# Routing operands of the later groups made tile by tile inside the shared expert's stages, first loads in program order, and the last two batches' rows stored by GpSimd, in a one-core adapter and mixture-of-experts kernel

## The chip, the core and the metric

The kernel runs on one core of a Trainium2 chip. A core has five engines with queues of their own: PE (matrix products), DVE (vector operations), ACT (casts, copies, activations), POOL (here mostly indirect transfers) and SP (which only issues transfers). Each engine works through its instructions in the order fixed when the kernel is built; an instruction that waits for a semaphore holds back all behind it on the same engine. The metric is the device time of one execution in microseconds, lower is better.

## The reference

Two parts in a row: a per-batch adapter product, then a feed-forward layer with a shared expert and 16 routed experts, of which each token uses two. The result is added to `x`.

```
x: (8, 256, 1024) f32;  itok: adapter id per batch (8 of them, here 3 to 7)
y = einsum('bsi,boi->bso', x, cond_weight[itok])        # 8 x [256,1024] x [1024,1024]
t = y.reshape(2048, 1024)
shared = (silu(t @ sg.T) * (t @ su.T)) @ shared_down.T   # 1024 -> 1024 -> 1024
p = softmax(t @ gate_w.T)                                # 16 experts
v, i = top_k(p, 2);  v = v / sum(v)
moe = sum over the two experts e in i of  v_e * ((silu(t @ g_e.T) * (t @ u_e.T)) @ w_down_e.T)   # inner size 256
out = x + shared + moe
```

The 2048 rows of `t` are handled as four groups of 512 rows (two batches each).

## The kernel before, in words

**Precision.** Every large fp32 operand is split into a high part (an ACT cast, L84) and a low remainder (a DVE subtraction, L85); `split` does both. `mm3` (L133) then makes a product out of three matmuls, high x high (L134), high x low (L135) and low x high (L136). So each operand costs one ACT and one DVE instruction of about 1.0 and 1.2 us per 128x1024 tile, and PE runs three matmuls for one product.

**Loads.** `load_w` (L114) issues one 512 KB load on SP into one of the `wst` staging buffers and splits it into one of five `whl` buffers; PE frees such a buffer with its last matmul on it. After each load `load_w` takes one entry from the hand-written list `between`, if there is one, and runs it right behind that split: this is how small pieces of other work are put among the large products. `held` and `after_loads` likewise tie work behind the last split or the last load. A scheduler at build time fixes the order on each engine, within those ties.

**First part of the span.** Twenty matmuls on a constant tile come first (L149). Then `cond(b)` for b = 0 to 7 makes the adapter product of a batch: two tiles of `xT` and eight weight tiles, 96 matmuls, copies of the sums into `yrow` by ACT (L270), and two stores of these rows to `y_d` in DRAM (L272, on ACT's queue). `load_first` (L100) cuts the first two tiles of batch 0 into halves so that PE may start sooner. `constants` (L171) fills small tables on POOL and DVE. The rows come back by POOL's fetch `yr<-y_d` (L394) and a DVE stream transpose (L218, `turned(b, k)` in the list), into `raw` for groups 0 and 1, and for groups 2 and 3 into `tt`.

**The shared expert's gate and up products** of groups 0 and 1 are made with a seven-product (Strassen-like) scheme, class `Up`, in stages a, b, c and d of four steps u each; `product` (L503) makes 24 matmuls of 128x512 a time. Stage c adds to copies of `X` put into the accumulators by ACT (`seeded`), its result goes into `G` by L574; stage d adds into `X` on DVE (L585), which also frees accumulators. Stage c needs the operand `t4`, stage d needs `t1` and `b22`, each two tiles of a ring (`operand_half`, L398). The stages alternate with `cond(4)` to `cond(7)`.

**Routing.** For each group the logits are 32 matmuls on operands that for groups 2 and 3 are made from `tt` into `whl` buffers named `rb`, in two halves (k = 0 and 1, one batch each) by `half_works` (L412): `operands` makes both tiles of a half, `products` runs its 16 matmuls (L278). `choices(g)` then runs `route` (L287): softmax and top two on DVE, rank matmuls `rk` (L339 to L349), places for each row. `scatter(g)` writes eight columns of row numbers to a table in DRAM with POOL's indirect transfers (L378).

**Behind the last group.** Experts are sorted by count on DVE, one indirect read brings the table back (L891, `cr`), a DVE transpose and addition make the row indices `ix` (L898), and POOL gathers the experts' rows with one indirect transfer per quarter tile (L805, in `expert_rows`). Meanwhile `shared_down` (L620) makes the shared expert's down product of groups 0 and 1. Each of the two has the rows of `x` loaded into `acc` tiles (L615; group 0 on SP's queue, group 1 on POOL's), adds the accumulators to them on DVE (L641), which frees the accumulators, and stores the sum (L642). After that come the 16 experts, then the shared expert for groups 2 and 3 and the last sums.

The order around the change is the program at the end of the kernel: `cond(5)`, stage b steps 2 and 3, `cond(6)`, stage c steps 0 and 1, `cond(7)`, stage c 2 and 3, stage d 0 to 3, `scatter(3)`.

Of the kernel before, what the change touches and what calls it, by code (L numbers as in the profile page):

```python
# [1 line left out]

# [8 lines left out]
FR = mybir.dt.float32r  # L11
# [6 lines left out]
P = 128  # L18
# [21 lines left out]
def adapter_moe_kernel(ctx: ExitStack, tc: tile.TileContext, xT, x, itok, wc, gate, wgu, wd, sgu, sd, out):  # L40
# [39 lines left out]

    last_cast, last_split, last_load = [None], [None], [None]

    def split(hi, lo, src):
        last_cast[0] = nc.scalar.copy(hi, src).ins  # L84
        last_split[0] = nc.vector.tensor_tensor(lo, src, hi.bitcast(F32), op=ALU.subtract).ins  # L85
        return last_split[0]


    def held(*works):
        with tc.issue_after(last_split[0]):  # L90
            for work in works:
                work()
# [21 lines left out]
    def load_w(src, staged=(wst, "wst")):  # L114
        st = staged[0].tile([P, 1024], F32, tag=staged[1], name="st")
        loads[0] += 1
        hl = homes[loads[0] % len(homes)].tile([P, 2, 1024], FR, tag="whl", name="hl")
        last_load[0] = nc.sync.dma_start(st, src)
        end = split(hl[:, 0, :], hl[:, 1, :], st)
        work = between.pop(0) if between else None  # L120
        if work:
            with tc.issue_after(end):
                work()
        return hl

    def after_loads(work):
        def later():
            with tc.issue_after(last_load[0].ins):
                work()

        return later
# [14 lines left out]

    nc.gpsimd.memset(ones, 1.0)
    warm = psm.tile([P, 4, P], F32, tag="sm", name="warm")
    for k in range(20):  # L149
        nc.tensor.matmul(warm, ones, ones[:, :].rearrange("p (o n) -> p o n", o=1).to_broadcast([P, 4, P]), start=True, stop=True)  # L150


# [85 lines left out]
    def cond(b, rows, staged=(wst, "wst")):  # L238
        aid = []

        def weights(k):
            if not aid:
                aid.append(nc.values_load(it_sb[0:1, b : b + 1], engines=(mybir.EngineType.SP,), min_val=0, max_val=NA - 1))
            return wc[ds(aid[0], 1), k].rearrange("a p f -> p (a f)")

        if b == 0:
            x0, w0 = load_first(lambda: xT[b, :, 0, :], lambda: weights(0), staged)
            xt = [x0]
        else:
            xt, w0 = [load_w(xT[b, :, 0, :], staged)], None  # L250
        yrow = [rows.tile([P, 1024], F32, tag="yrow", name=f"yrow{k}") for k in range(2)]
        for h in range(2):
            ps = [bank() for k in range(2)]
            for q in range(4):
                if h == 0 and q == 2:
                    xt.append(load_w(xT[b, :, 1, :], staged))
                w = w0 if w0 and h == q == 0 else load_w(weights(h * 4 + q))
                for k in range(2):
                    for ci in range(2):
                        c = 2 * q + ci  # L260
                        xv = xt[c // 4].rearrange("p l (c s) -> p l c s", c=4)
                        mm3(
                            ps[k],
                            [xv[:, l, c % 4, k * P : (k + 1) * P] for l in range(2)],
                            [w[:, l, ci * 512 : (ci + 1) * 512] for l in range(2)],
                            c == 0,
                            c == NC - 1,
                        )
            for k in range(2):
                nc.scalar.copy(yrow[k][:, h * 512 : (h + 1) * 512], ps[k])  # L270
        for k in range(2):
            nc.scalar.dma_start(y_d[2 * b + k].rearrange("a p f -> p a f"), yrow[k][:, :].rearrange("p (a f) -> p a f", a=4))  # L272


    def route_part(lp, n0, get, n):
        for c in range(NC):
            for l in range(2):
                nc.tensor.matmul(  # L278
                    lp[:, n0 : n0 + n],
                    gpk[:, c * 2 * E : c * 2 * E + P],  # L280
                    get(c)[l],
                    start=(c == 0 and l == 0),
                    stop=(c == NC - 1 and l == 1),
                )
# [86 lines left out]
    def scatter(g):  # L371
        with tc.issue_after(last_rows[0]):
            scatter_now(g)
# [29 lines left out]
    def operand(ring, src):  # L403
        return [operand_half(ring, src, k) for k in range(2)]
# [7 lines left out]
    def half_works(g, k, src):  # L412
        t = []

        def operands():
            for q in range(2):
                rb = whl.tile([P, 2, 4, 2 * P], FR, tag="whl", name="rb")
                split(rb[:, 0], rb[:, 1], src[:, 4 * q : 4 * q + 4, :])
                t.append(rb)

        def products():
            if k == 0:
                lps[g] = logits()
            with tc.issue_after(last_product[0]):
                route_part(lps[g], k * 2 * P, lambda c: [t[c // 4][:, l, c % 4, :] for l in range(2)], 2 * P)

        return operands, products

    def choices(g):
        return lambda: route(g, lps[g])  # L430

# [7 lines left out]
    def logits():  # L439
        return psm.tile([P, GT], F32, tag="sm", name="lp")  # L440

    def both(*works):
        def work():
            for w in works:
                w()

        return work
# [2 lines left out]

    class Up:
        def __init__(self, first, raw, X, S, G, ring, ys, g0):
            self.first, self.raw, self.X, self.S, self.G, self.ring, self.ys, self.g0 = first, raw, X, S, G, ring, ys, g0
            if first:
                s, at = ([a[:, 2 * k : 2 * k + 2, :].rearrange("p a n -> p (a n)") for k in range(a.shape[1] // 2)] for a in (S, self.half(0, 0)))
                self.spare = [s, s, s[2:] + at, [s[3]] + at + [None]]
# [96 lines left out]
        def stage_b(self, u, made=False):  # L553
# [8 lines left out]
            for m in range(2):  # L562
                self.product(ps[m], w2, m, self.t3, False)
                nc.scalar.copy(self.X[:, 2 * u + m, :], ps[m])

        def stage_c(self, u):
            if u == 0:
                self.t4 = operand(self.ring, self.half(1, 0))
            w = load_w(sgu[1, 1, u])
            ps = self.seeded(u)  # L570
            for m in range(2):
                f = 2 * u + m
                self.product(ps[m], w, m, self.t4, False)
                nc.vector.tensor_tensor(self.G[:, f, :], self.G[:, f, :], ps[m], op=ALU.mult)  # L574

        def stage_d(self, u):
            if u == 0:
                self.t1 = operand(self.ring, self.half(0, 1))
                self.b22 = operand(self.ring, self.half(1, 1))
            w1, w2 = load_w(ss_d[0, u]), load_w(ss_d[3, u])  # L580
            ps = [bank() for m in range(2)]
            for m in range(2):
                f = 2 * u + m
                self.product(ps[m], w1, m, self.t1, True)
                nc.vector.tensor_tensor(self.X[:, f, :], ps[m], self.X[:, f, :], op=ALU.add)  # L585
            if u:
                self.end_d()
            self.open = u, ps, w2
            if u == 3:
                self.end_d()  # L590
# [360 lines left out]
    def fetch_rows(b, dst):  # L951
        def work():
            rows[b] = batch_rows(b, ys, dst)

        return work

    def turned(b, k):
        return lambda: rows[b][k]()

    cond(0, ys, early)  # L960
    fetch_rows(0, up.place(0, 0))()
    constants(ring)
    cond(1, ys, early)
    between[:] = [turned(0, 0), None, both(turned(0, 1), fetch_rows(1, up.place(0, 1))), after_loads(lambda: tables(ring))]
    cond(2, ys)
# [25 lines left out]
    cond(4, ys)  # L991
    tv = tt.rearrange("p k (b n) -> p (k b) n", b=4)
    fetch_rows(4, tv)()
    h0, h1 = half_works(2, 0, tv), half_works(2, 1, tv)
    up.sums_operands()
    between[:] = [None, choices(1)]
    up.stage_b(0)
# [1 line left out]
    ws = up.sums_weights(2)  # L999
    between[:] = [ws[0], turned(4, 0)]  # L1000
    up.stage_b(1)
    between[:] = [ws[1], turned(4, 1), None, h0[0], None, h0[1]]
    cond(5, ys)
    after_loads(lambda: up.sums_fetch(3))()
    up.stage_b(2)
    fetch_rows(5, tv)()
    held(*up.sums_weights(3))
    up.stage_b(3, True)
    between[:] = [turned(5, 0), None, turned(5, 1), None, h1[0], h1[1], None, choices(2)]
    cond(6, ys)  # L1010
    fetch_rows(6, tv)()
    scatter(0)
    scatter(1)
    h0, h1 = half_works(3, 0, tv), half_works(3, 1, tv)
    up.stage_c(0)
    up.stage_c(1)
    between[:] = [None, None, turned(6, 0), None, turned(6, 1), None, h0[0], h0[1]]
    cond(7, ys)
    fetch_rows(7, tv)()
    scatter(2)  # L1020
    up.stage_c(2)
    up.stage_c(3)
    up.stage_d(0)
    between[:] = [None, turned(7, 0)]
    up.stage_d(1)
    between[:] = [both(turned(7, 1), h1[0]), h1[1]]
    up.stage_d(2)
    between[:] = [None, choices(3)]
    up.stage_d(3)
    scatter(3)  # L1030
    close(px, pr)
# [282 lines left out]
```

## Time and profile before

| | us |
|---|---|
| median of 3 runs | 994.86 (992.32 to 999.79) |
| the profiled execution | 995.32 |
| its span | 993.1 |
| PE busy | 976.3 (98%) |
| DVE busy | 704.0 (71%) |
| ACT busy | 543.0 (55%) |
| POOL busy | 331.4 (33%) |
| granted TensorE clock, mean | 0.994 |

By stage, PE is busy 11.65 of the first 15 us, all of 15 to 195 us (the adapter products of the first batches and stage a), 142.39 of the 150 us to 345 (batches 5 to 7 among stages b, c, d), all of 345 to 755 (the shared expert's first down products, from which the row gathers start, then the experts), and 232.30 of the last 238.1.

How to read it: the span runs from the first instruction to the last. An engine's busy share is an average over stages that have different limits; what a piece of work is worth is read from the stage where it lies, from the idle time ahead of PE's instructions and from the instruction that ended it. In the timeline a row gives start, duration, engine, line, operation with output and input, shape, and in brackets the idle time before it with what ended it.

### The profile page before, as it was taken

Reading aid. Unit: us, or ns where it says so; the run is one execution under the profiler, and the core shown is the slowest. Engines: PE = TensorE matmul, PEld = TensorE weight load, DVE = VectorE, ACT = ScalarE, POOL = GpSimd, SP = SyncE. Lnnn points to the kernel's source line nnn. Section 1 sums busy time; section 2 is a strip of 40 time slices with the busy share of each in tenths; the row PEclk is TensorE's granted clock in tenths of the full one; section 3 lists DMA queues with packets and bytes.
Section 4 is the critical chain, followed back from the end, with each engine's and each line's share of the span. In section 5 each row is a group of like instructions: output and inputs, shape, how many; then the busy total and the mean of one; then the engine's idle time right before and its main releaser. Section 6 shows DMA issues by size and latency. Waiting matters only on the chain.

```text
span 993.1 us, 14073 instructions
## 1 busy us (share of the span) xinstructions
PE 976.3 (98%) x5012; PEld 833.6 (84%) x5012; DVE 704.0 (71%) x931; ACT 543.0 (55%) x729; POOL 331.4 (33%) x334
## 2 busy tenths in 40 slices
PE   8999999999999899999999999999999999999997
PEld 5888888878878688889999999999998888888886
DVE  5566888846855785947788787778777654968782
ACT  4555646546735352323767777777774566425450
POOL 2000200101052303763888887545000323241600
PEclk9999999999999999999999999999999999999999
DMA  8899968958678745687878888878886989995952
GB/s 287 281 332 350 367 211 283 345 197 292 197 227 224 186 122 119 192 311 234 284 255 312 301 293 293 287 272 305 279 312 221 324 301 296 347 266 130 252 160 100
DMA packets 84205, 256.94 MB, mean 259 GB/s; under 512 B 13084, under 2 KB 21420, under 8 KB 84124
## 3 DMA queue, kind: packets, MB, share of 16 engines
q1 hardware_dynamic: 50508, 174.48, 52.4%
q0 software_dynamic: 22480, 71.89, 22.7%
q10 hardware_dynamic: 11136, 9.57, 2.9%
q8 instruction: 41, 0.67, 0.3%
q14 instruction: 40, 0.33, 0.1%
HBM read 207.62 MB, written 48.28 MB: 258 GB/s over the span
## 4 chain that ended last, share of the span: by engine, by line
PE 91%; DMA 4%; DVE 1%; ACT 1%; issue 1%; SPq 0%; ACTq 0%; POOLq 0%; DVEq 0%
PE acc L503 28%; PE acc L135 18%; PE acc L136 18%; PE acc L134 17%; PE acc L697 8%; PE acc L873 2%; DMA yr<-y_d 1%; PE lp L278 1%; DMA st<-ss_d 1%; DVE hl L85 1%; DMA st<-wc 1%; ACT hl L84 1%; DMA y_d<-yrow 1%; DMA st<-sgu 1%; DVE op L85 0%
## 5 line engine op out<-in xcount | busy, mean ns | idle before, releaser
L85 DVE TENSOR_TENSOR hl<-st,hl 128x1024 fp32r<-128x1024 f32 (+1 forms) x254 | 304.7, 1209 | 150.7 <-ACT hl L84 132.8
L84 ACT CAST hl<-st 128x1024 fp32r<-128x1024 f32 (+1 forms) x254 | 263.0, 1043 | 203.2 <-PE acc L136 91.0
L503 PE MATMUL acc<-op,hl 128*128 128x512 f32 x1296 | 299.6, 391 | 4.1 <-DVE X L585 4.1
L503 PEld LDWEIGHTS acc<-op,hl 128*128 128x128 f32 x1296 | 243.6, 189 | 55.6 <-issue 4.5
L805 POOL DMA_INDIRECT yg<-y_d,ix x128 | 185.1, 1446 | 81.5 <-issue 35.0
L136 PE MATMUL acc<-yte,hl 128*128 128x256 f32 (+6 forms) x512 | 147.3, 288 | 0.0
L134 PE MATMUL acc<-yte,hl 128*128 128x256 f32 (+6 forms) x512 | 147.1, 288 | 0.0
L135 PE MATMUL acc<-yte,hl 128*128 128x256 f32 (+6 forms) x512 | 147.0, 287 | 0.0
L135 PE MATMUL acc<-hl 128*128 128x512 f32 x256 | 101.6, 397 | 2.9 <-DVE hl L85 2.8
L136 PE MATMUL acc<-hl 128*128 128x512 f32 x256 | 101.1, 395 | 0.0
L135 PEld LDWEIGHTS acc<-yte,hl 128*128 128x128 f32 x512 | 96.5, 188 | 0.6
L134 PEld LDWEIGHTS acc<-yte,hl 128*128 128x128 f32 x512 | 96.3, 188 | 0.6
L136 PEld LDWEIGHTS acc<-yte,hl 128*128 128x128 f32 x512 | 96.2, 188 | 0.0
L134 PE MATMUL acc<-hl 128*128 128x512 f32 x256 | 91.3, 395 | 3.0 <-ACT hl L84 3.0
L394 POOL DMA_DIRECT2D yr<-y_d x16 | 8.8, 553 | 173.6 <-DMA y_d<-yrow 92.4
L135 PEld LDWEIGHTS acc<-hl 128*128 128x128 f32 x256 | 48.7, 190 | 15.2 <-DVE hl L85 5.0
L134 PEld LDWEIGHTS acc<-hl 128*128 128x128 f32 x256 | 48.0, 190 | 14.5 <-ACT hl L84 4.9
L136 PEld LDWEIGHTS acc<-hl 128*128 128x128 f32 x256 | 48.9, 191 | 10.3
L378 POOL DMA_INDIRECT tab_d<-tid,places x32 | 35.8, 1118 | 50.1 <-DVE ranks L364 40.6
L135 PE MATMUL acc<-hl,at 128*128 128x512 f32 x128 | 49.9, 390 | 0.0
L134 PE MATMUL acc<-hl,at 128*128 128x512 f32 x128 | 49.9, 390 | 0.0
L134 PE MATMUL acc<-hl,ht 128*128 128x512 f32 x128 | 49.9, 390 | 0.0
(229 smaller groups left out, 1400.8 us busy)
## 6 DMA issues: line engine op xcount, KB each, us to landing
st<-wgu SPq DMA_DIRECT2D x64, 512.0 KB
st<-wc SPq DMA_DIRECT2D x63, 512.0 KB
st<-wd SPq DMA_DIRECT2D x32, 512.0 KB
os_d<-o SPq DMA_DIRECT2D x32, 512.0 KB
st<-ss_d SPq DMA_DIRECT2D x30, 512.0 KB
st<-sd SPq DMA_DIRECT2D x30, 512.0 KB
st<-sgu SPq DMA_DIRECT2D x24, 512.0 KB
yr<-y_d POOLq DMA_DIRECT2D x20, 512.0 KB
```

What stands on the lines that cost most here:

```text
L84: last_cast[0] = nc.scalar.copy(hi, src).ins
L85: last_split[0] = nc.vector.tensor_tensor(lo, src, hi.bitcast(F32), op=ALU.subtract).ins
L134: nc.tensor.matmul(ps, lhs[0], rhs[0], start=first, stop=False)
L135: nc.tensor.matmul(ps, lhs[0], rhs[1], start=False, stop=False)
L136: last_product[0] = nc.tensor.matmul(ps, lhs[1], rhs[0], start=False, stop=last).ins
L278: nc.tensor.matmul(lp[:, n0 : n0 + n], gpk[:, c * 2 * E : c * 2 * E + P], get(c)[l], start=(c == 0 and l == 0), stop=(c == NC - 1 and l == 1),
L378: i = nc.gpsimd.indirect_dma_start(out=tab_d[:, :], out_offset=bass.IndirectOffsetOnAxis(ap=places[r][:, tb : tb + 1], axis=0), in_=tid[r] ...
L394: last_rows[0] = nc.gpsimd.dma_start(r, y_d[tb].rearrange("a (i t) f -> (a i) (t f)", t=4)).ins
L503: last_product[0] = nc.tensor.matmul(ps, lhs[x], rhs[y], start=(first and c == 0 and i == 0), stop=(c == 3 and i == 2), skip_group_check=T ...
L697: nc.tensor.matmul(ps[k], lhs[x], rhs[y], start=(first and t == c == i == 0), stop=(t == c == 1 and i == 2), skip_group_check=True,)
L805: last_gather[0] = nc.gpsimd.indirect_dma_start(out=r[:, t * 256 : (t + 1) * 256], out_offset=None, in_=y_d.rearrange("k a p f -> (k a p) f"),
L873: nc.tensor.matmul(ps, a3[:, fi, :], w[fi][:, l, hs], start=(fi == 0 and l == 0), stop=(fi == 1 and l == 1))
```

## The change

The number of opening matmuls goes from 20 to 16. While `in_order[0]` is set, which it is until `cond(0)` is through, each load of `load_w` is issued behind the one before it in the program. `constants` is tied behind the last split of `cond(0)`. The stores of `yrow` go to POOL's queue for batches 6 and 7. `half_steps` takes the place of `half_works` for groups 2 and 3 (`half_works` stays in use for group 1): three steps, the first tile's operands; its eight products and the second tile's operands; the last eight products. The steps are put into the stages b, c and d and the first loads of `cond(6)` and `cond(7)`, as the list at the end of the diff says, and `choices(2)` and `choices(3)` with them. The operands `t4` and `t1` are made by entries of the list in `cond(6)` and at stage c step 3, where before they were made at the start of stages c and d.

```diff
--- before.py
+++ after.py
@@ -1,4 +1,4 @@
-from contextlib import ExitStack
+from contextlib import ExitStack, nullcontext
 
 import concourse.bass as bass
 import concourse.tile as tile
@@ -80,6 +80,8 @@
 
     last_cast, last_split, last_load = [None], [None], [None]
 
+    in_order = [True]
+
     def split(hi, lo, src):
         last_cast[0] = nc.scalar.copy(hi, src).ins
         last_split[0] = nc.vector.tensor_tensor(lo, src, hi.bitcast(F32), op=ALU.subtract).ins
@@ -115,7 +117,8 @@
         st = staged[0].tile([P, 1024], F32, tag=staged[1], name="st")
         loads[0] += 1
         hl = homes[loads[0] % len(homes)].tile([P, 2, 1024], FR, tag="whl", name="hl")
-        last_load[0] = nc.sync.dma_start(st, src)
+        with tc.issue_after(last_load[0].ins) if in_order[0] else nullcontext():
+            last_load[0] = nc.sync.dma_start(st, src)
         end = split(hl[:, 0, :], hl[:, 1, :], st)
         work = between.pop(0) if between else None
         if work:
@@ -146,7 +149,7 @@
 
     nc.gpsimd.memset(ones, 1.0)
     warm = psm.tile([P, 4, P], F32, tag="sm", name="warm")
-    for k in range(20):
+    for k in range(16):
         nc.tensor.matmul(warm, ones, ones[:, :].rearrange("p (o n) -> p o n", o=1).to_broadcast([P, 4, P]), start=True, stop=True)
 
 
@@ -269,11 +272,11 @@
             for k in range(2):
                 nc.scalar.copy(yrow[k][:, h * 512 : (h + 1) * 512], ps[k])
         for k in range(2):
-            nc.scalar.dma_start(y_d[2 * b + k].rearrange("a p f -> p a f"), yrow[k][:, :].rearrange("p (a f) -> p a f", a=4))
-
-
-    def route_part(lp, n0, get, n):
-        for c in range(NC):
+            (nc.gpsimd if b > 5 else nc.scalar).dma_start(y_d[2 * b + k].rearrange("a p f -> p a f"), yrow[k][:, :].rearrange("p (a f) -> p a f", a=4))
+
+
+    def route_part(lp, n0, get, n, chunks=range(NC)):
+        for c in chunks:
             for l in range(2):
                 nc.tensor.matmul(
                     lp[:, n0 : n0 + n],
@@ -426,6 +429,24 @@
 
         return operands, products
 
+
+    def half_steps(g, k, src):
+        t = []
+
+        def operands():
+            t.append(whl.tile([P, 2, 4, 2 * P], FR, tag="whl", name="rb"))
+            q = len(t) - 1
+            split(t[q][:, 0], t[q][:, 1], src[:, 4 * q : 4 * q + 4, :])
+
+        def products():
+            q = len(t) - 1
+            if k == q == 0:
+                lps[g] = logits()
+            with tc.issue_after(last_product[0]):
+                route_part(lps[g], k * 2 * P, lambda c: [t[q][:, l, c % 4, :] for l in range(2)], 2 * P, range(4 * q, 4 * q + 4))
+
+        return operands, both(products, operands), products
+
     def choices(g):
         return lambda: route(g, lps[g])
 
@@ -450,6 +471,7 @@
 
     class Up:
         def __init__(self, first, raw, X, S, G, ring, ys, g0):
+            self.t1 = self.t4 = None
             self.first, self.raw, self.X, self.S, self.G, self.ring, self.ys, self.g0 = first, raw, X, S, G, ring, ys, g0
             if first:
                 s, at = ([a[:, 2 * k : 2 * k + 2, :].rearrange("p a n -> p (a n)") for k in range(a.shape[1] // 2)] for a in (S, self.half(0, 0)))
@@ -563,8 +585,14 @@
                 self.product(ps[m], w2, m, self.t3, False)
                 nc.scalar.copy(self.X[:, 2 * u + m, :], ps[m])
 
+
+        def operand_work(self, name, k, n):
+            t = []
+            setattr(self, name, t)
+            return [lambda q=q: t.append(operand_half(self.ring, self.half(k, n), q)) for q in range(2)]
+
         def stage_c(self, u):
-            if u == 0:
+            if u == 0 and not self.t4:
                 self.t4 = operand(self.ring, self.half(1, 0))
             w = load_w(sgu[1, 1, u])
             ps = self.seeded(u)
@@ -574,8 +602,9 @@
                 nc.vector.tensor_tensor(self.G[:, f, :], self.G[:, f, :], ps[m], op=ALU.mult)
 
         def stage_d(self, u):
+            if u == 0 and not self.t1:
+                self.t1 = operand(self.ring, self.half(0, 1))
             if u == 0:
-                self.t1 = operand(self.ring, self.half(0, 1))
                 self.b22 = operand(self.ring, self.half(1, 1))
             w1, w2 = load_w(ss_d[0, u]), load_w(ss_d[3, u])
             ps = [bank() for m in range(2)]
@@ -958,8 +987,9 @@
         return lambda: rows[b][k]()
 
     cond(0, ys, early)
+    in_order[0] = False
     fetch_rows(0, up.place(0, 0))()
-    constants(ring)
+    held(lambda: constants(ring))
     cond(1, ys, early)
     between[:] = [turned(0, 0), None, both(turned(0, 1), fetch_rows(1, up.place(0, 1))), after_loads(lambda: tables(ring))]
     cond(2, ys)
@@ -991,7 +1021,7 @@
     cond(4, ys)
     tv = tt.rearrange("p k (b n) -> p (k b) n", b=4)
     fetch_rows(4, tv)()
-    h0, h1 = half_works(2, 0, tv), half_works(2, 1, tv)
+    h0, h1 = half_steps(2, 0, tv), half_steps(2, 1, tv)
     up.sums_operands()
     between[:] = [None, choices(1)]
     up.stage_b(0)
@@ -999,33 +1029,41 @@
     ws = up.sums_weights(2)
     between[:] = [ws[0], turned(4, 0)]
     up.stage_b(1)
-    between[:] = [ws[1], turned(4, 1), None, h0[0], None, h0[1]]
+    between[:] = [ws[1], turned(4, 1)]
     cond(5, ys)
     after_loads(lambda: up.sums_fetch(3))()
+    between[:] = [h0[0]]
     up.stage_b(2)
     fetch_rows(5, tv)()
-    held(*up.sums_weights(3))
+    held(*up.sums_weights(3), h0[1])
     up.stage_b(3, True)
-    between[:] = [turned(5, 0), None, turned(5, 1), None, h1[0], h1[1], None, choices(2)]
+    t4 = up.operand_work("t4", 1, 0)
+    between[:] = [h0[2], turned(5, 0), None, None, turned(5, 1), None, t4[0], None, t4[1]]
     cond(6, ys)
     fetch_rows(6, tv)()
     scatter(0)
     scatter(1)
-    h0, h1 = half_works(3, 0, tv), half_works(3, 1, tv)
+    g2 = h1
+    h0, h1 = half_steps(3, 0, tv), half_steps(3, 1, tv)
+    between[:] = [g2[0]]
     up.stage_c(0)
+    between[:] = [g2[1]]
     up.stage_c(1)
-    between[:] = [None, None, turned(6, 0), None, turned(6, 1), None, h0[0], h0[1]]
+    between[:] = [g2[2], choices(2), None, None, turned(6, 0), None, turned(6, 1)]
     cond(7, ys)
     fetch_rows(7, tv)()
     scatter(2)
+    t1 = up.operand_work("t1", 0, 1)
+    between[:] = [h0[0]]
     up.stage_c(2)
+    between[:] = [both(h0[1], *t1)]
     up.stage_c(3)
+    between[:] = [h0[2]]
     up.stage_d(0)
-    between[:] = [None, turned(7, 0)]
     up.stage_d(1)
-    between[:] = [both(turned(7, 1), h1[0]), h1[1]]
+    between[:] = [turned(7, 0), both(turned(7, 1), h1[0])]
     up.stage_d(2)
-    between[:] = [None, choices(3)]
+    between[:] = [h1[1], both(h1[2], choices(3))]
     up.stage_d(3)
     scatter(3)
     close(px, pr)
```

## The prediction

> **What bounds the kernel.** I first read busy time by stage (columns: stage, its length, then busy us of PE, PEld, DVE, ACT and POOL, granted TensorE clock, DMA share, GB/s).
>
> ```profile
> 15.00:195.00 180.00, 180.00 (x819) 148.42 (x818) 133.57 (x190) 104.97 (x129) 15.51 (x28) 1.00 0.88 313
> 195.00:345.00 150.00, 142.39 (x637) 116.15 (x636) 93.06 (x124) 77.22 (x95) 32.38 (x34) 0.97 0.70 217
> 345.00:460.00 115.00, 115.00 (x520) 94.63 (x519) 77.26 (x157) 38.43 (x41) 43.14 (x41) 1.00 0.61 188
> ```
>
> PE bounds every stage but one: from 195 to 345 us it misses 7.6 us of busy time and some of its clock. A change pays only by removing PE idle time there, in the first 15 us, or in matmul count. Second, PE's waits (total, times, longest) name the releasers:
>
> ```profile
> PE acc L503 <- DVE X L585: 4.1, 1, 4.1
> PE acc L134 <- ACT hl L84: 3.0, 3, 1.3
> PE acc L135 <- DVE hl L85: 2.8, 3, 1.8
> ```
>
> Third, the timeline around each (start, duration, engine, instruction, the idle time before it and its releaser):
>
> ```profile
> 196.73 2.16 ACT L84 CAST rb<-tt 128x1024 fp32r<-128x1024 f32 x2
> 200.54 1.04 ACT L84 CAST hl<-st 128x1024 fp32r<-128x1024 f32 x1 [1.65 <-PE acc L136]
> 201.64 0.73 PE L134 MATMUL acc<-hl 128*128 128x512 f32 x2 [1.18 <-ACT hl L84]
> ...
> 284.80 1.25 DVE L218 STREAM_TRANSPOSE tt<-yr 128x1024 f32<-128x1024 f32 x1 [6.38 <-DMA yr<-y_d]
> 287.80 0.50 PE L135 MATMUL acc<-hl 128*128 128x512 f32 x1 [1.77 <-DVE hl L85]
> ...
> 308.70 1.06 ACT L270 COPY yrow<-acc 128x512 f32<-128x512 f32 x2
> 313.50 1.05 ACT L84 CAST hl<-st 128x1024 fp32r<-128x1024 f32 x1 [3.73 <-DMA st<-ss_d]
> 314.83 1.08 ACTq L272 DMA_DIRECT2D y_d<-yrow  x2
> 326.61 1.25 DVE L218 STREAM_TRANSPOSE tt<-yr 128x1024 f32<-128x1024 f32 x1 [6.44 <-DMA yr<-y_d]
> 333.70 3.47 PE L503 MATMUL acc<-op,hl 128*128 128x512 f32 x8 [4.07 <-DVE X L585]
> ```
>
> Each stall has a story. First (200 us): two routing casts took two of the five weight buffers, so the next weight cast waited until PE freed one. Second (286 us): DVE sat 6.4 us at a transpose whose rows had not landed; the split behind it came late. Third (329 us): ACT had the last batch's rows copied at 309.8 but stored them only at 314.8, behind a cast that waited for its load; the rows came late, DVE stood 6.4 us, and the X addition behind came late.
>
> I measure a stall as start-to-start time above the warm 0.227 us of a 128x512 matmul: 1.34+0.69, then 1.93, then 4.23+0.33, and 0.3 at 222 and at 299 us: 9.1 us. After each of the three, seven matmuls start 0.427 us apart: 3 x 7 x 0.20 = 4.2, and with rounding about 0.4 us of partly slowed ones. Together **13.7 us**.
>
> **Part 1, stages.** Routing of groups 2 and 3 now takes one weight buffer at a time and its products run in 8s inside stages b, c, d. Matmuls, casts and splits keep their number and size; their engines had room (ACT 77 of 150 us busy, DVE 93). With the removed stalls subtracted from all times, I walked each moved item against its need. First stall: the two casts no longer precede batch 5's loads; its casts gain at least 2.5 us of slack, so it goes whole. Second: batch 6's rows need to be in by about 279, and land about 277 (store 262.3, 8 us to land, 6.7 to fetch); gone, with 2 us to spare. Late next are one hl split about 0.5 us (246.5 against 246.0) and single buffer waits; no row shows them, so 0 to 3 (one more stall of the second's kind); I charge 0.9, nearest to what the walk gives.
>
> **Part 2, Pool stores.** Two issues per batch, 0.37 and 0.52 us on ACT, become Pool issues (a plain 512 KB fetch there takes 0.55). Batch 7's copies end at about 297.5 on the new axis. Pool is then past the 16 index scatters of groups 0 and 1 (16 x about 1.3 us from 271, done by 292.7), so the rows are stored about 298, land 304.7, are fetched by 312.2 and transposed by 315.9; PE needs X at 324.1. So the third stall goes, with 6 us to spare. The Trainium skill speaks against this part: "DMA: Bandwidth & Descriptors", section "SWDGE vs HWDGE vs iDMA", gives plain transfers to SP or ACT, as Pool's descriptors are built in software. In rows the price is at most 0.2 us an issue; against it ACT's store waited 5 us. By the rule alone I would call the third stall's 5.9 us unchanged (net 0.4 instead of 6.3); the rows win, as the margin covers the difference.
>
> **Part 3, start.** Ahead of the first weights went a 512 KB xT half that is not needed until the third weight tile. At the page's 287 to 367 GB/s it is 1.4 to 1.8 us of queue; the first weight cast waits 2.50 us for its load. Gain 1.4 (bounds 0, if the transfers' fixed time limits, and 2.5). Sixteen warm matmuls end near 6.9, and starts 0.427 us apart end at 5.65, so the clock stays up: 0. DVE's three constants (under 4 us) go behind batch 0's last split; nothing needs them until routing. SP is moved past no wait, only its order of loads.
>
> **Part 4, the tail of routing.** The last group's choices move behind its last 8 products, and 40 matmuls further in PE's stream (157 instead of 197 lie between its rank matmuls and the combine step): 40 x 0.227 = 9.1 us less time for everything behind:
>
> ```profile
> 374.72 0.20 PE L339 MATMUL rk<-mk,tri 128*128 128x64 bf16 x1
> 393.31 0.99 POOL L891 DMA_INDIRECT cr<-tab_d,column  x1 [5.53 <-issue]
> 400.25 0.97 POOL L805 DMA_INDIRECT yg<-y_d,ix  x1 [5.95 <-ACT hl L84]
> 431.77 1.72 POOL L615 DMA_DIRECT2D acc<-x  x3
> 436.54 0.69 DVE L641 TENSOR_TENSOR acc<-acc,acc 128x512 f32<-128x512 f32 x1 [2.51 <-DMA acc<-x]
> ```
>
> This is a serial line on Pool: 8 scatters, the table read, 22 row gathers (31.5 us, 1.43 each with the 0.30 between them), and only then group 1's x rows (L615), which DVE adds before PE may reuse that accumulator. Before, PE wanted the bank near 440.6 and had it at 437.4: 3.2 us of slack. Now the line is 9.1 + 0.6 (one hl split falls between its two DVE steps) - 3.2 = 6.5 us late, and seven matmuls at 0.427 follow: **7.9**, all on PE's path. Queued behind the late addition on DVE are weight splits PE also needs; that is inside the 6.5. This does not depend on how much the early stages gain: both ends of it move with them.
>
> The rule that bears on the clock: "TensorE: Matmul & The Clock Gate", section "What's actually happening", says the clock halves only after an idle window of some 3.4 us. The rows differ: idles of 1.77 us and of 1.18+0.53 us were followed by seven starts at 0.427 us. By the rule the first two stalls are worth 2.8 less: 3.5 net; by the rows 6.3. The rows stand.
>
> **Sum.** 13.7 + 1.4 - 0.9 - 7.9 = 6.3. Profiled execution 995.3 (span 993.1 and 2.2 around it) gives 989.0; the median of the runs, 994.86, lies 0.46 lower: **988.5**. From here 1% (about what a measurement of this kernel can tell from no change) is 984.9 to 1004.8.
>
> **Rivals.** (A) *The Pool line is on time*: gathers at their usual shortest (0.96 + 0.30 = 1.26) save 22 x 0.17 = 3.7, and an earlier sort or x fetch the rest. Then the gain is 14.2: 980.7. For: most gathers are 0.96 long. Against: nothing in the change shortens the line by the 6.5 needed; half of it gives 985.
> (B) *Slower: the gathers stretch.* Over the whole kernel their mean is 1.446, so 1.75 with the gap. At that, 22 x 0.32 = 7.0 more, and it lands wholly on PE: 995.5; at the longest I see in this line, 1.81 to 1.95, about 11.5 more: 1000. It decides from 0.29 us a gather on (6.3/22). Against: DMA share is 0.77 where they run, below the experts' 0.84.
> (C) *The third stall stays*: Pool is held past 304 by scatters or a fetch, so stores come as late as ACT's did: 988.5 + 5.9 = 994.4.
> (D) *The first stalls reappear elsewhere* (buffers, 3.6 each): 992 to 996.
>
> **Chances.** My forecast 0.50, A 0.26 (with its halves), B 0.12, C 0.06, D 0.06. My forecast's own range is 985 to 992. For 8 in 10, I go down past A to 979.5 and up past C and the cheaper B to 997. Faster by over 1%: A without its halves' upper end, and the forecast's lower edge: 0.28. Slower by over 1% needs B far beyond its seen mean, or B with C: 0.10. Within: 0.62.
>
> **What would show it.** Right: no PE wait over 1 us between 190 and 330; the third one's L585 release gone; L272's stores on Pool issued within 1 us of the copies; first weight matmul near 7; one new PE wait for DVE L641 (L644 in the new numbering) of 4 to 7 us near 430, after a POOL x-row issue. Wrong: that wait absent (A), gathers' mean over 1.4 without gap (B), yr fetches still ahead of a DVE idle of 6 us (C).

## The result and the profile after

| | before | changed |
|---|---|---|
| median of 15 runs each, us | 993.29 | 990.30 |
| ratio to before, 95% interval | | 0.9963 (0.9945 to 0.9981) |
| span of the profiled execution, us | 993.1 | 989.2 |
| PE busy, us | 976.3 | 974.3 |

The change saves 0.37%, 3.7 us of 993.29 by the ratio (1.9 to 5.5): beyond the noise, and some 60% of the forecast 6.3. Busy time by stage in the changed kernel, columns as before:

```profile
0.00:15.00 15.00, 11.86 (x36) 6.20 (x37) 5.91 (x7) 7.31 (x9) 5.33 (x54) 0.95 0.75 253
...
195.00:345.00 150.00, 149.78 (x696) 124.45 (x695) 101.56 (x142) 81.10 (x99) 40.43 (x38) 1.00 0.78 231
345.00:460.00 115.00, 109.98 (x495) 90.15 (x494) 73.73 (x153) 38.47 (x41) 45.89 (x44) 0.97 0.62 184
```

The 7.6 us hole between 195 and 345 is gone (149.78 of 150 us busy, clock back to 1.00), and a hole of 5.0 us has opened in the stage behind it, which had none. The first row shows a granted clock of 0.95, where it was 1.00. PE's waits name the new releaser (line numbers are those of the changed kernel; L670 is what L641 was):

```profile
PE acc L137 <- DVE acc L670: 5.0, 2, 4.2
PE acc L137 <- ACT hl L86: 1.6, 1, 1.6
PE acc L138 <- DVE hl L87: 1.4, 3, 0.6
```

The old first row (X, 4.1 us) is gone. What is left of the two others lies outside the stage but for 0.2 us: the 1.6 is one wait at 11.8 us, and of the 1.4, 0.5 lies at 13 us, 0.65 at 62 and 0.2 at 248. The timeline of the last rank matmuls and around the two new waits:

```profile
371.86 0.20 PE L342 MATMUL rk<-mk,tri 128*128 128x64 bf16 x1
...
407.54 1.25 DVE L221 STREAM_TRANSPOSE tt<-yg 128x1024 f32<-128x1024 f32 x1 [3.75 <-DMA yg<-y_d,ix]
410.13 0.68 DVE L670 TENSOR_TENSOR acc<-acc,acc 128x512 f32<-128x512 f32 x1
410.87 0.80 PE L137 MATMUL acc<-hl,ht 128*128 128x512 f32 x1 [4.22 <-DVE acc L670]
...
430.83 2.23 POOL L644 DMA_DIRECT2D acc<-x  x4
435.92 0.69 DVE L670 TENSOR_TENSOR acc<-acc,acc 128x512 f32<-128x512 f32 x1 [7.18 <-DMA acc<-x]
436.67 0.50 PE L137 MATMUL acc<-hl,ht 128*128 128x512 f32 x1 [0.80 <-DVE acc L670]
```

The late Pool line hits PE twice. At 410.9 PE waits for an addition of group 0 whose data had long been there: it stands on DVE behind a transpose that waits for gathered rows (the bracket of the second row) and a split that follows it. At 436.7 it waits for group 1's addition, which waits for x rows that POOL issued behind 22 gathers.

Matmul starts give the balance. Lost time is here the sum of what start-to-start times exceed 0.227 us by, counted where it is over 0.1 us. From 190 to 345 us it fell from 13.65 to 0.60, and from 400 to 440 us it rose from 0.11 to 8.10 (4.4 and 1.0 of waiting, the rest starts at half clock, nearly all between the two waits). The last piece is the start. Two product matmuls of the kernel before, the first of all and the 12th:

```profile
8.26 0.73 PE L134 MATMUL acc<-hl 128*128 128x512 f32 x2 [0.50 <-ACT hl L84]
...
12.89 0.73 PE L134 MATMUL acc<-hl 128*128 128x512 f32 x2 [1.31 <-ACT hl L84]
```

In the changed kernel they come at 7.12 and 11.83, over 1 us earlier; then starts at half clock follow (rows in experiment 6), and the first matmul of batch 1 comes at 33.41 instead of 32.87. After one more stall of 0.9 us at 61 us PE is 1.4 us behind. 13.05 - 7.99 - 1.4 = 3.7; the spans differ by 3.9, as the count leaves out the starts that are late by less than 0.1 us.

### The profile page after: what moved, and what is told of

It is laid out like the page before. It is cut to its first block, busy times and chain, and to the rows that moved or that the text cites. A ratio compares the mean times of both kernels' runs of the same rounds, so it can differ in the third digit from the quotient of the medians.

```text
span 989.2 us, 14071 instructions
## 1 busy us (share of the span) xinstructions
PE 974.3 (98%) x5008; PEld 833.3 (84%) x5008; DVE 704.0 (71%) x931; ACT 544.2 (55%) x729; POOL 320.3 (32%) x338
## 4 chain that ended last, share of the span: by engine, by line
PE 55%; POOL 2%; DMA 2%; issue 2%; DVE 0%; ACT 0%; DVEq 0%; POOLq 0%
PE acc L525 15%; PE acc L137 10%; PE acc L139 10%; PE acc L138 10%; PE acc L726 8%; PE acc L902 2%; POOL yg L834 1%; DMA yg<-y_d,ix 1%; DMA acc<-x 1%; POOL tab_d L381 0%; DMA cr<-tab_d,column 0%; POOL yl L834 0%; DVE tt L221 0%; DVE hl L87 0%; ACT yte L86 0%
## 5 line engine op out<-in xcount | busy, mean ns | idle before, releaser
L834 POOL DMA_INDIRECT yg<-y_d,ix x128 | 167.3, 1307 | 78.7 <-issue 31.7
L381 POOL DMA_INDIRECT tab_d<-tid,places x32 | 40.6, 1267 | 57.9 <-DVE ranks L367 48.5
L138 PEld LDWEIGHTS acc<-hl 128*128 128x128 f32 x256 | 48.5, 189 | 12.8 <-DVE hl L87 2.7
L137 PE MATMUL acc<-hl,ht 128*128 128x512 f32 x128 | 51.2, 400 | 5.0 <-DVE acc L670 5.0
L138 PE MATMUL acc<-hl,ht 128*128 128x512 f32 x128 | 50.7, 396 | 0.0
L139 PE MATMUL acc<-hl,ht 128*128 128x512 f32 x128 | 50.7, 396 | 0.0
```

What stands on the lines that cost most here:

```text
L137: nc.tensor.matmul(ps, lhs[0], rhs[0], start=first, stop=False)
L138: nc.tensor.matmul(ps, lhs[0], rhs[1], start=False, stop=False)
L139: last_product[0] = nc.tensor.matmul(ps, lhs[1], rhs[0], start=False, stop=last).ins
L381: i = nc.gpsimd.indirect_dma_start(out=tab_d[:, :], out_offset=bass.IndirectOffsetOnAxis(ap=places[r][:, tb : tb + 1], axis=0), in_=tid[r] ...
L834: last_gather[0] = nc.gpsimd.indirect_dma_start(out=r[:, t * 256 : (t + 1) * 256], out_offset=None, in_=y_d.rearrange("k a p f -> (k a p) f"),
```

## The experiments

Theory: the stages are mended whole, and one late line on POOL gives back 8 us at two places. Each ratio is to the kernel before, timed beside it on the same chip; that kernel's own median moved between 991.5 and 996.3 us from chip to chip, so the ratios are compared and not the times.

**1. Additions ahead of the transposes.** The first expert's rows are tied behind group 0's additions:

```diff
-    between[:] = [None, weights, works[0], x_rows, ...]
+    def after_sums(work, end=last_sum[0]):
+        def later():
+            with tc.issue_after(end):
+                work()
+        return later
+    between[:] = [None, weights, after_sums(works[0]), x_rows, ...]
```

> The changed kernel, with the first expert's row transposes tied behind group 0's four additions into acc (nothing on DVE waits for a gather ahead of them any more). Theory (the Pool line of gathers and x rows sets the end of this stage, whatever waits first): the 4.2 us PE wait near 406 us goes, the 0.8 us wait near 435 us grows to 5 to 7 us, one half-clock stretch instead of two; time within 2 us of the changed kernel's 990.3, at best 988.5. Rival (the queue on DVE is the cause by itself): the 406 us wait goes and nothing takes its place; 6 us less, about 984.

Ratio 0.9967 (0.9951 to 0.9983), the changed kernel's. The one wait left at L670, in this version's timeline:

```profile
426.66 0.61 POOL L644 DMA_DIRECT2D acc<-x  x1
431.56 0.69 DVE L670 TENSOR_TENSOR acc<-acc,acc 128x512 f32<-128x512 f32 x1 [6.98 <-DMA acc<-x]
432.31 0.50 PE L137 MATMUL acc<-hl,ht 128*128 128x512 f32 x1 [3.02 <-DVE acc L670]
```

The first wait is gone and the second has grown from 0.8 to 3.0 us: PE came earlier to the place where POOL is late. (It grew less than the 5 to 7 expected; the first x row was issued 4 us earlier, at 426.7. In this profile PE lost 5.0 us from 400 to 440, not 8.1, and 1.1 more at 459 in waits for casts, so a gain of a microsecond or two that the timings do not show is not ruled out.) The queue on DVE is one of two catches, not the cause by itself.

**2. x rows ahead of the second expert's gathers,** alone (`last_x` is the last of the four loads):

```diff
-    rs = expert_rows(pa[1], 1)
     acc, x_rows = down_rows(1, ys, nc.gpsimd)
-    between[:] = [None, weights, works[0], x_rows, works[1], None, works[2]]
+    x_rows()
+    with tc.issue_after(last_x[0]):
+        rs = expert_rows(pa[1], 1)
+    between[:] = [None, weights, works[0], None, works[1], None, works[2]]
```

> The changed kernel, with group 1's four x-row loads issued on POOL ahead of the second expert's gathers instead of behind its first ones; DVE's order as in the changed kernel. Theory: the wait near 435 us (0.8 us) goes, the one near 406 us (4.2 us) and its half-clock matmuls stay; about 1 us less, 989. Rival (x rows behind the gathers are the whole cause): both waits go, 8 us less, 982.

```profile
PE acc L137 <- DVE acc L670: 4.5, 1, 4.5
```

The waits are as the theory said (one of 4.5 us, at 412, none at L670 behind it), the time is not: 1.0001 (0.9983 to 1.0018), slower than the changed kernel. Its profile has 4 us of PE pauses with no releaser near 447 and 520 us, and the latest start of all. So I ran the same edit with the first loads free of program order:

> The version with the x rows early alone (DVE's order as in the changed kernel), with the first loads free of program order. Theory (its slow result was its slow start and stalls without a releaser in the profile): wait for L670 near 406 us of 4 to 5 us, none near 435, ratio 0.993 to 0.9965, like the changed kernel's. Rival (x rows ahead of the gathers hold something up by themselves): ratio 0.998 or more, with a new named wait behind 415 us.

0.9939 (0.9916 to 0.9962), with one wait of 2.6 us at L670 near 408 (expected 4 to 5) and none later. So the edit by itself does not slow the kernel; what made all fourteen runs of the first version slow stays open. Nor does the edit gain much: its fair partner is the changed kernel with free loads (experiment 6), at 0.9947, with 6.3 us lost from 400 to 440 us against 4.4 here.

**3. Both.**

> Both edits together: additions ahead of the first expert's transposes on DVE, and x rows ahead of the second expert's gathers on POOL. Theory (two places in a row on one late line, each of which catches what the other lets through): neither wait is left, no half-clock stretch after 400 us; 8 us less than the changed kernel, about 982. Rival: the gathers of the first experts, now later, hold PE at the first expert (a wait of 3 us or more behind 440 us); 985 to 990.

0.9898 (0.9869 to 0.9928), 986.36 against 996.30. PE's waits in its profile:

```profile
PE acc L137 <- ACT hl L86: 2.4, 1, 2.4
PE acc L138 <- DVE hl L87: 1.5, 3, 0.8
PE acc L139 <- issue: 1.4, 2, 1.0
PE acc L138 <- issue: 0.8, 1, 0.8
```

No row names L670, and lost time from 400 to 440 us is 0.11. The four rows are the start, small splits, and pauses near 442 us that no releaser explains. The rival had foreseen a wait behind 440 us, for late gathers; the two later profiles with the same edits (experiment 6) have no named wait over 0.5 us between 440 and 460, so these pauses do not come with the edits. The timeline of this version shows why no wait at L670 is left (rows of acc and tt only):

```profile
405.82 1.88 DVE L670 TENSOR_TENSOR acc<-acc,acc 128x512 f32<-128x512 f32 x3
407.62 1.23 DVE L221 STREAM_TRANSPOSE tt<-yg 128x1024 f32<-128x1024 f32 x1
412.05 1.18 POOL L644 DMA_DIRECT2D acc<-x  x2
```

The additions come first, the accumulators and `acc` tiles are free by then, and the x rows leave 19 us sooner. One edit alone brings nothing that the times can tell (1: 0.9963 to 0.9967; 2, with free loads: 0.9947 to 0.9939), both together about 6.5 us (0.9963 to 0.9898). With free loads both bring 3.8 (0.9947 to 0.9909, intervals that just touch). Two catches on one late line.

**4. Group 3 whole,** with `half_works` and the slots that it had before (`choices(3)` at the second load of stage d step 3), group 2 still in steps:

```diff
-    h0, h1 = half_steps(3, 0, tv), half_steps(3, 1, tv)
+    h0, h1 = half_works(3, 0, tv), half_works(3, 1, tv)
...
```

> The changed kernel with group 3's routing as it was before (half_works, two operand tiles at once, choices at stage d step 3 second load), all else as changed: the last rank matmuls are back at their old place, 40 matmuls earlier in PE's stream. Theory: the waits for L670 near 406 and 435 us go (8 us with their half-clock matmuls), and the squeeze of weight buffers costs 0 to 4 us of new PE waits in batch 7 or stage d; 982.5 to 986.5. Rival (the later place of the rank matmuls is not what makes the line late): the waits at L670 stay above 3 us, 990 or more.

0.9938 (0.9918 to 0.9958). The waits at L670 are gone (0.11 us lost from 400 to 440): the later place of group 3's routing, its rank matmuls at the end, makes the line late. But the squeeze costs 5.8 us, more than the 0 to 4 expected (4.66 from 260 to 300 us, 1.17 to 345):

```profile
292.04 0.73 PE L137 MATMUL acc<-hl 128*128 128x512 f32 x2 [1.13 <-ACT hl L86]
293.56 0.20 PE L342 MATMUL rk<-mk,tri 128*128 128x64 bf16 x1 [0.79 <-DVE oh L324]
294.80 0.50 PE L138 MATMUL acc<-hl 128*128 128x512 f32 x1 [0.93 <-DVE hl L87]
```

So group 3's steps save 5.8 us at one end and cost 8.0 at the other, and the kernel with group 2's alone is as fast or faster.

**5. Who removed the third stall?** First, the changed kernel with its stores back on ACT (`nc.scalar` for all batches):

> The changed kernel with the rows of batches 6 and 7 stored on ACT's queue as before; PE's, DVE's and SP's orders are the same, and on ACT the second store of each batch stands behind one weight cast. Theory (the stages, not the queue, removed the third stall, and the rows have some 6 us to spare): no new PE wait over 1 us between 300 and 345 us; within 0.2% of the changed kernel (ratio to the kernel before 0.9945 to 0.998). Rival (the Pool stores are what removed it): a PE wait of about 4 us behind L614 comes back, 6 us with its half-clock matmuls; ratio 1.001 or more.

0.9961 (0.9948 to 0.9973): the same, with no loss from 300 to 345 us. Its two stores of batch 7, and those of the changed kernel:

```profile
298.03 0.37 ACTq L275 DMA_DIRECT2D y_d<-yrow  x1
299.16 0.37 ACTq L275 DMA_DIRECT2D y_d<-yrow  x1
```

```profile
300.16 1.60 POOL L275 DMA_DIRECT2D y_d<-yrow  x2
```

With the new stages no cast that waits for a load stands ahead of ACT's stores any more: each follows its copy at once. ACT stores no later than POOL (PE was some 1 us ahead here, from its start). Then the other way round, the kernel before with Pool stores and nothing else:

> The kernel before with nothing changed but the stores of batches 6 and 7, now on POOL. Theory: the rows of batch 7 are stored near 311 instead of 314.8, the transposes on DVE come 4 us earlier, and the PE wait of 4.1 us for L585 shrinks to below 1.5; the waits at 200 and 286 us stay; 3 to 6 us less, ratio 0.994 to 0.997. Rival (the stage order decides): the 4.1 us wait stays above 3, ratio 0.999 to 1.001.

0.9947 (0.9916 to 0.9977): this one line gains about as much as the whole change. Its stores and the first transpose of batch 7:

```profile
312.04 1.60 POOL L272 DMA_DIRECT2D y_d<-yrow  x2 [13.90 <-ACT yrow L270]
325.68 1.25 DVE L218 STREAM_TRANSPOSE tt<-yr 128x1024 f32<-128x1024 f32 x1 [1.55 <-DMA yr<-y_d]
```

From the last copy (312.3, before 309.8) to this transpose it is 13.4 us instead of 16.8. The wait for X is gone and the loss from 300 to 345 us falls from 5.72 to 1.97, but 260 to 300 us rises from 3.86 to 6.87 (waits at routing products and the cast behind them, partly pauses without a releaser); this one execution took 995.32 us, where the median of nine was 988.34, so its losses are not typical. Either part removes the third stall; both together do not remove it twice.

**6. The start.** The changed kernel with its loads free of program order (`in_order = [False]`):

> The changed kernel with the first loads free again to be issued before their turn (one line), so that the xT half goes ahead of the first weights; PE, DVE and ACT orders unchanged, 16 opening matmuls. Theory: first product matmul at 7.9 to 8.6 instead of 7.1 us; with only 16 opening matmuls an idle stretch of over 1 us ahead of it, so the clock is no better kept: 96th product matmul 0.5 to 2 us later than with the loads in order (33.4 in the changed kernel's trace). Rival (the load order itself brought the half-clock matmuls of the start): fewer than 3 starts 0.427 us apart between 7 and 20 us, 96th product matmul at 32.9 or earlier.

0.9947 (0.9927 to 0.9968), if anything faster than with the order, and its trace is the rival's: first product at 7.81, 96th at 31.92, no half-clock starts. My theory, that 16 opening matmuls leave PE idle too long, fell here. The kernel before with the new start alone:

> The kernel before with the start of the changed one alone (16 opening matmuls, first loads in program order, constants behind the first batch's last split); the stages as before. Theory, from the other traces (first product matmul 0.9 to 1.9 us earlier, but the 12th at the same time, because the second whole weight tile lands no earlier, and half-clock starts behind that longer wait): a wait of 1.6 us or more for the cast before the 12th matmul, and no gain: ratio 0.9985 to 1.002. Rival (the sum of the prediction): 1.4 us gained and kept to the end, 96th matmul at 31.5, ratio 0.997 to 0.9985.

0.9999 (0.9984 to 1.0014): the start earns nothing, though its wait before the 12th matmul was 0.8 us, not 1.6. Both tail edits with 20 opening matmuls:

> The version with both tail edits (additions first, x rows early) and 20 opening matmuls again instead of 16. Theory (fewer opening matmuls leave PE idle longer inside the clock's first windows): no half-clock starts between 7 and 20 us, first product matmul near 7.8 us, 96th at 32.0 to 32.8; 0 to 1.5 us less than with 16, ratio 0.9885 to 0.990. Rival (it is chance where the windows fall): half-clock starts here as well, 96th at 33 or later.

0.9891 (0.9866 to 0.9916), the same as with 16. Half-clock starts (5) came here too, and the 96th at 34.60: again the rival's case, so that fewer opening matmuls are not what brings them. And both tail edits with free loads, which has the lowest median seen (on the chip on which the kernel before is fastest too):

> The version with both tail edits and 16 opening matmuls, with the first loads free of program order again. Theory: no PE wait for L670 and no half-clock stretch after 400 us as with both edits, 96th matmul near 32, no half-clock starts before 20 us; ratio 0.987 to 0.9895. Rival (the old order gains nothing on the mean): ratio 0.9895 to 0.9905, 96th matmul above 32.8.

0.9909 (0.9888 to 0.9930), 982.72 against 991.48: the ratio is outside the theory's range and just outside the rival's, while the 96th at 32.57 and the clean trace fit the theory. The interval covers the versions with ordered loads, so that the order of the loads is worth less than these timings can tell. Its trace loses 0.3 us between 260 us and the end. Each of the thirteen profiles has one of two orders of loads, and together they say more than the times (product matmuls counted from 0, times in us):

```
loads     profiles   first   12th    96th (first of batch 1)   with 5 to 9 half-clock starts by 20 us
free          5       8.01   12.40   32.38                     0 of 5
in order      8       6.91   12.25   33.38                     5 of 8
```

In order, the first product comes on the mean 1.1 us earlier, but the 12th gains only 0.15: it needs the second weight tile, which on the mean lands hardly earlier. The gain turns into a longer wait for that tile's cast (0.8 to 1.3 us became, in seven of eight, 1.6 to 3.4), and behind that wait the clock dropped in five of the seven:

```profile
11.83 0.73 PE L137 MATMUL acc<-hl 128*128 128x512 f32 x2 [1.61 <-ACT hl L86]
...
13.69 0.63 PE L137 MATMUL acc<-hl 128*128 128x512 f32 x1
14.12 0.63 PE L138 MATMUL acc<-hl 128*128 128x512 f32 x1
```

In these rows of the changed kernel starts lie 0.43 us apart; with free loads (experiment 6, first run) the same place shows

```profile
11.95 0.73 PE L137 MATMUL acc<-hl 128*128 128x512 f32 x2 [0.82 <-ACT hl L86]
...
13.78 0.39 PE L137 MATMUL acc<-hl 128*128 128x512 f32 x1
14.01 0.40 PE L138 MATMUL acc<-hl 128*128 128x512 f32 x1
```

and starts 0.23 us apart.

What decides is in the traces too. In all thirteen the granted clock changes only on a grid of 3.413 us: between its first rise and the very end every stretch at half clock lasts 3.41 or 6.83 us, and the stretches at full clock between them are whole multiples (in the kernel before 198.0, 81.9 and 41.0 us, which is 58, 24 and 12 steps). The grid lies differently in each profile; the first rise to full clock, between 4.4 and 7.0 us, shows where. Steps of this grid (columns as in the first table), in the changed kernel:

```profile
10.20:13.62 3.42, 1.28 (x5) 0.78 (x5) 1.98 (x3) 2.45 (x3) 0.00 (x0) 1.00 1.03 418
13.62:17.03 3.41, 3.41 (x9) 2.63 (x8) 3.12 (x3) 1.73 (x2) 0.00 (x0) 0.50 1.01 399
```

and with both tail edits (experiment 3):

```profile
7.83:11.24 3.41, 1.93 (x9) 1.25 (x7) 0.69 (x1) 0.76 (x2) 0.00 (x0) 1.00 0.89 357
11.24:14.66 3.42, 1.93 (x7) 1.32 (x8) 2.46 (x3) 3.01 (x3) 0.00 (x0) 1.00 1.04 420
14.66:18.07 3.41, 3.41 (x16) 2.80 (x16) 3.22 (x3) 2.11 (x2) 0.00 (x0) 1.00 0.95 358
```

In the first, 2.1 us of PE's idle time lie in one step, and the next runs at half clock. In the second the wait is longer (2.4), but the border of two steps cuts it, each has 1.5 us of idle time, and the clock stays up. From the first rise to 20 us before the end the thirteen profiles have 3631 steps at full clock. Half clock follows on 18 of them, and these have 1.71 us of idle time or more; of all the others one has 1.90, the rest at most 1.49. So in these runs idle time of about half a step is what halves the clock for the next. Loads in order lengthen the wait past that, and the place of the grid, which differs from profile to profile, decides whether it counts.

## Why the prediction was right, step by step

The median came out at 990.30, within the forecast's own range of 985 to 992 and 1.8 above its 988.5. Part of that is luck: the forecast started from 994.86, a median of three runs, where fifteen gave 993.29; a gain of 6.3 from there would have been 987.0.

- **The early stalls (13.7 less 0.9).** Right: 13.05 net was measured against 12.8; of the 0.9 charged, only a wait of 0.2 at 248 us came. No run parts the half steps from the earlier making of `t4` and `t1`.
- **Pool stores.** The third stall went, but not through this step. The prediction gave it 5.9 us and set the rule against plain stores on POOL aside because "ACT's store waited 5 us"; under the new stages that wait on ACT does not exist, and the stores on ACT do as well (0.9961 against 0.9963). The error was to cost a part against the old schedule of the other part. The 0.2 us an issue charged to POOL was too small to be seen either way.
- **The start (+1.4).** This is the step that failed. It put the clock at 0, as the opening starts 0.427 us apart had ended at 5.65. In the profile the first product came 1.14 us earlier and the 12th 1.06, but the wait before the 12th grew from 1.3 to 1.6, and nine starts at half clock behind it cost 1.6: -0.5 by batch 1. Over the thirteen profiles even the gain to the 12th is only 0.15. The step took "the queue is shorter" for "PE is ahead" without asking what PE needs next. With the start alone the time did not fall either (0.9999, experiment 6). The further 0.9 us at 61 us was not foreseen; it is there with free loads too (0.93), so it is not the order's.
- **The tail (7.9).** Right in size (8.0 more than before) and in the late line, wrong in where it is caught: most of the waiting is at group 0's additions behind the gather's transpose (4.4, not foreseen), only 1.0 at group 1's (L670; the L644 of the prediction is the x-row load). The size is right in part by luck. The last rank matmuls start at 371.86 (timeline above), 2.9 us earlier than before, while PE is 11.9 ahead: 9 us late, as forecast. From there to the x rows it took 59.0 us instead of 57.1, 1.9 more where the step had put 0.6; but the 1.4 for half-clock starts behind the last wait did not come (0.1), and those between the waits cost nothing of their own, as PE had to wait for the x rows anyway. Gathers kept their pace, 32.0 us for 22, 1.455 each against 1.43, so the slower rival fell (its upper edge left out the 0.30 us between gathers: 22 x (1.81 + 0.30 - 1.43) is 15, not 11.5); nothing shortened the line by enough, so the faster one fell.
- **The sum.** 12.8 + 1.4 - 7.9 = 6.3 was forecast; 13.05 - 1.4 - 8.0 = 3.7 came. The missing 2.6 us is the start's 1.9 (from +1.4 to -0.5) and the 0.9 at 61 us, less the 0.2 that the stages gave beyond the forecast.
- **The clock rule.** The prediction took the rows against the threshold of 3.4 us. The measured 3.7 lies near the 3.5 that it gave by the rule, but only by accident: the early stalls gave 13.05, where the rule leaves 12.8 - 2.8 = 10.0. The grid of experiment 6 shows why the rows were right: a step need not be wholly idle. The idle times at 201 and at 288 us (1.18 + 0.53 and 1.77) each lie in one step, and half clock followed; near 11 us waits of 2.2 (stores on ACT) and 2.4 (both edits) were cut by a border, and it did not. The same section of the Trainium skill ("TensorE: Matmul & The Clock Gate", "What's actually happening") says that the window is free-running; the grid, whose place differs from profile to profile, agrees with that.

## What to carry to other kernels

When work is moved later to relieve one stage, follow its results to the last reader: here 9 us of delay in a few tiny matmuls came out 39 us later as a wait of PE for an unrelated addition. A late line that has two catches needs both taken away: mending one moved the wait and saved no time that could be told. Short waits of PE close together can cost its clock as well: here 1.7 us within one step of 3.4 were enough. And cost each part of a change against the schedule that the other parts make, else two of them are credited with the same stall.

## What was not expected

Half the experiments' profiles have stretches in which PE pauses for 0.2 to 1.3 us several times with no releaser, for instance 2.2 us near 444 in the version with both edits and 2.0 near 449 in that with x rows early; the profiles of the kernels before and after have none, and the places differ from run to run. Their cause stays open; in one profile they cost as much as the whole change saves (4 us), so that a single profile cannot rank these versions.
